# Layer 2's attention: a layer norm issued in halves between the counting exponentials, and v placed by two copies

## Chip, cores and metric

The kernel runs on one core of a Trainium2 chip. The metric is the device time of one execution in microseconds (us). The engines are PE (the matrix engine, with PEld for its weight loads), DVE (vector engine), ACT (scalar engine), POOL (GpSimd) and SP, which issues DMAs. Each engine works through its own queue in order.

## What is computed

Four layers, each a cross attention over a context and then a feed-forward part, act on `x` of 128 batches x 64 positions x 128 channels, all in float32. Each result is added to `x` with a tanh gate. Only layer 2's attention is touched by the change. Cut to what matters:

```python
q = (layernorm(x) @ Wq + bq)      # 16 heads of 8 channels
k = (ctx @ Wk + bk); v = (ctx @ Wv + bv)
attn = clip(einsum('bhqd,bhkd->bhqk', q, k) * 8 ** -0.5, -1e4, 1e4)
attn = softmax(attn)
attn = where(any(isnan(attn)), 1 / Nkv, attn)
x = x + tanh(g) * (einsum('bhqk,bhkd->bqhd', attn, v) @ Wo + bo)
```

The test for NaN runs over the whole tensor, so it is taken after all scores exist. The kernel forms it with an extra exponential of the raw scores, summed per row into `cnt`.

## The kernel before

**Tiling.** The 8192 tokens are 64 tiles of 128. Layer 2's attention works on 32 units of two tiles (`NP`, argument `u`) and 16 groups of four tiles (`NG`, argument `g`); a group is two units. An even unit is the first of its group.

**The steps of a group.** `statistics` (L786) takes mean and variance on DVE and, on POOL, four small operations that give `rr` (one over the deviation) and `nb` (minus mean times `rr`). `norm` (L798) applies both on ACT, one instruction for each of four tiles, into `xn`, of which there is a single buffer; then POOL adds the gated bias `b2` to the group's `x` in place. `transposes` (L806) turns `xn` on PE, `qk` (L813) forms q and k.

**The steps of a unit.** `spread` (L824, POOL) spreads k over head slots into `kb`; `scores` (L832, PE) fills two two-bank tiles `sc[0]` and `sc[1]`; `count` (L843, ACT) is the extra exponential, once for each of them; `clamp` (L848, DVE) clips each into `s`; `largest` (L855, DVE) takes the row maxima; `less` (L859, POOL, two halves) subtracts them; `power` (L863, ACT, two halves) is the softmax's exponential; `values` (L867, PE) forms v in `psv`; `place` (L876, DVE) copies v from there into a zeroed tile `vz`, in which each head's 8 columns sit at their own offset; `turn` (L886) transposes the exponentials on PE and copies them to `aT` on ACT; `heads` (L896, PE) multiplies them with `vz` and with a 0/1 tile that yields the row sums; `divide` (L913, DVE) makes the quotient.

**Order.** Steps of several units are interleaved by a list written out by hand, `PLAN` (L920). `period(i)` (L927) walks it once: an entry `("u", lag, f, ...)` calls `f` for unit `i + lag`, an entry `("g", lag, f)` calls it for group `(i + lag) / 2` when `i + lag` is even. The wrapper `InOrder` chains the instructions of every engine in the order in which they are issued, so an instruction that waits holds back all later ones of its engine. Before the change the list begins with count 0, clamp 1, clamp 0, count 1 of unit `i`, and ends with `("g", 6, statistics), ("g", 5, norm)`. So `statistics` of a group is the last step of an even unit, and its `norm` is the last step of the following odd unit. POOL's queue in an even unit is: the two `less`, the two multiplications of `spread`, the four small operations of `statistics`; in an odd unit: two `less`, two of `spread`, and the bias.

**Buffers.** One-bank PSUM tiles (L63) rotate over four banks: `psx`, `psq`, `psk`, `psv`, `psa` and `pso` share them. The two `sc` tiles (L66) are the only two of their kind, so the next unit's `scores` waits until `count` and `clamp` of the present one have read both.

**Around it.** Periods -6 to -2 run while layer 1 still works; the loop proper starts at -1. Layer 2's feed-forward part follows.

Of the kernel before, what the change touches and what calls it, by code (L numbers as in the profile page):

```python
# [9 lines left out]
F32 = mybir.dt.float32  # L10
# [3 lines left out]
ALU = mybir.AluOpType  # L14
AX = mybir.AxisListType

P = 128
# [37 lines left out]
def flamingo_kernel(ctx: ExitStack, tc: tile.TileContext, a: dict, out: bass.AP):  # L55
# [7 lines left out]
    def bank(name):  # L63
        return psum.tile([P, 512], F32, tag="one", name=name, bufs=4)
# [23 lines left out]
    x = const.tile([P, NT, DM], F32, name="x")  # L88
# [45 lines left out]
    def gated_bias(key):  # L134

        if key not in gbias:
            n = dict(b0=0, b1=1, b1f=5, b2=2, b3f=7, go=3)[key]
            gbias[key] = const.tile([P, DM], F32, name=f"gbias_{key}")
            dve.tensor_scalar(gbias[key], row[key], tg[:, n:n + 1], None, ALU.mult)
        return gbias[key]  # L140
# [5 lines left out]
    def bc(ap, axis, n):  # L146

        shape = list(ap.shape)
        shape.insert(axis, n)
        return ap.unsqueeze(axis).to_broadcast(shape)  # L150
# [21 lines left out]
    dve, actor, gps, mat, sp = engines = [InOrder(e) for e in (vec, act, pool, pe, nc.sync)]  # L172

    def opened(name, bufs=1, side=None):
        pl = tc.tile_pool(name=name, bufs=bufs, side=side, reuse_waits="tile")
        return pl
# [568 lines left out]
    def l2_cross(ahead):  # L745
# [4 lines left out]
        wk = early.enter_context(opened("l2x_0", 2, RIGHT))  # L750
# [6 lines left out]
        v = keep.tile([P, 4, 4, 2, 32], F32, name="vz")  # L757
# [17 lines left out]
        ps = bank("psvm")  # L775
# [4 lines left out]
        sg, su = [{} for _ in range(NG)], [{} for _ in range(NP)]  # L780
# [14 lines left out]
            gps.tensor_tensor(nb, mv[:, :, 0], rr, ALU.mult)  # L795
            gps.tensor_scalar(nb, nb, -1.0, None, ALU.mult)

        def norm(g):  # L798
            xn = sg[g]["xn"] = wk.tile([P, 4, P], F32, tag="xn", name=f"xn_l2x_{g}", bufs=1)
            for t in range(4):  # L800
                actor.activation(xn[:, t, :], x[:, 4 * g + t, :], AF.Identity, bias=sg[g]["nb"][:, t:t + 1],
                                 scale=sg[g]["rr"][:, t:t + 1])
            xs = x[:, 4 * g:4 * g + 4, :]
            gps.tensor_tensor(xs, xs, bc(gated_bias("b2"), 1, 4), ALU.add)

        def transposes(g):  # L806
            ps = bank(f"psx_l2x_{g}")
# [68 lines left out]
        def place(u):  # L876
            ps = su[u]["psv"]
            for r in range(2):
                rows = slice(r * 64, r * 64 + 64)
                flat = v[rows].rearrange("p b c j m -> p (b c j m)")  # L880
                for j in range(2):
                    o0 = 48 * j + 8 * r
                    dve.tensor_copy(flat.rearrange("p (n m) -> p n m", m=64)[:, :, o0:o0 + 8],
                                    ps[rows, 0:256].rearrange("p (n j d) -> p n j d", j=2, d=8)[:, :, j, :])

        def turn(u, t):  # L886
            aT = su[u]["aT", t] = wk2.tile([P, 8, P], F32, tag="aT", name=f"aT_l2x_{u}_{t}")
# [25 lines left out]
        def divide(u):  # L913
# [4 lines left out]


        PLAN = [  # L920
            ("u", 0, count, 0), ("u", 0, clamp, 1), ("u", 0, clamp, 0), ("u", 0, count, 1),
            ("u", -3, heads), ("g", 3, qk), ("u", -1, power, 0), ("u", -1, power, 1),
            ("u", -2, values), ("u", -2, turn, 0), ("u", 1, scores), ("u", -2, turn, 1), ("g", 4, transposes),
            ("u", 0, largest), ("u", 0, less, 0), ("u", 0, less, 1), ("u", -2, place), ("u", 2, spread),
            ("u", -3, divide), ("g", 6, statistics), ("g", 5, norm),
        ]
        def period(i):  # L927
            for kind, lag, f, *more in PLAN:
# [454 lines left out]
    def ahead(n):  # L1383
# [4 lines left out]
        l0_ffn(ahead(1)),  # L1388
        cross("l1x", 1, "b1", False, "l2f", ahead(2), NP - 6, mixed=True),
        l2_cross(ahead(3)),  # L1390
        l2_ffn(ahead(4)),
        l3_cross(ahead(5)),
# [105 lines left out]
```

## Time and profile before

| | |
|---|---|
| runs shown | 3167.32, 3157.87, 3159.76 us; median 3159.76 |
| profiled execution | 3154.1 us, of which the span from first to last instruction is 3152.3 |
| busy in the span | PE 2984.2 (95%), PEld 1972.2, DVE 1935.9 (61%), ACT 1564.0 (50%), POOL 1261.6 (40%) |
| mean granted TensorE clock | 0.986 |
| layer 2's attention, counts of unit 0 to unit 31 | starts at 1297.88 to 1568.81 us |
| one pair of units in its steady part | 17.96 us (count 0 of even units at 1330.48, 1348.46, 1366.42, ... 1528.04) |
| count 0 to count 0, even unit to odd, odd to even | 6.88 and 11.08 us |
| one count, one clamp, one `largest` | 1.02, 1.22, 2.29 us |
| one half of `less`, one power, one aT copy | 1.90, 1.05, 0.59 us |
| one place copy (64 partitions x 128) | 0.28 us |

Times in the trace count from the first instruction. A row of the timeline gives the start, the length, the engine, the operation with what it writes and reads, and in brackets how long the engine had been idle before it and whose result ended that. `x2` at its end means that two like instructions are merged into the row. Every instruction is recorded at one helper's line (L166), so rows are told apart by the names of their tiles: `junk` is a count, `s<-sc` a clamp, `m` the maxima, `s<-s,m` is `less`, `s<-s` a power, `kb` is `spread`, `xn` is `norm`, `vz` is `place`.

### The profile page before, as it was taken

What the parts mean: (1) busy time and instruction counts of PE and PEld (TensorE: products, weight loads), DVE (VectorE), ACT (ScalarE), POOL (GpSimd) and SP (SyncE); (2) the same over time, 40 slices, a digit from 0 to 9 for tenths busy, and PEclk for the clock granted to TensorE, in tenths of its full rate; (3) what the DMA queues carried; (4) which work ended last, traced back from release to release, by engine and by line L of the source; (5) the groups of instructions that cost most, each with busy time, mean ns of one, the idle gap of its engine ahead of it and who ended that gap; (6) DMA issues with size and microseconds to landing.
All of it is one profiled execution on the core that took longest, in us unless ns stands there. A gap on an engine that the chain in (4) does not pass through costs nothing. (4 is left out here: it accounts for less than half of the span.)

```text
span 3152.3 us, 80010 instructions
## 1 busy us (share of the span) xinstructions
PE 2984.2 (95%) x34018; PEld 1972.2 (63%) x34018; DVE 1935.9 (61%) x4558; ACT 1564.0 (50%) x2756; POOL 1261.6 (40%) x1439
## 2 busy tenths in 40 slices
PE   8999899999989999778879999999999999999998
PEld 7888544444448888555654444444446888888883
DVE  5666666666546667699964544544545666666664
ACT  5666432232236666688822332332325666666655
POOL 3434311111014444787714444444443333333343
PEclk9999999999999999899989999999999999999998
DMA  5000455655510000000025335435430000000001
GB/s 151 2 3 2 109 135 120 137 122 124 132 51 3 3 2 2 29 3 2 2 55 109 83 80 109 82 81 109 87 77 14 2 2 2 3 2 3 2 3 54
DMA packets 89512, 164.93 MB, mean 52 GB/s; under 512 B 8929, under 2 KB 20833, under 8 KB 88193
## 3 DMA queue, kind: packets, MB, share of 16 engines
q1 hardware_dynamic: 89154, 159.81, 22.6%
q8 instruction: 267, 4.37, 0.6%
q14 instruction: 91, 0.75, 0.1%
HBM read 154.00 MB, written 5.77 MB: 51 GB/s over the span
## 5 line engine op out<-in xcount | busy, mean ns | idle before, releaser
L166 PE MATMUL psgu_l2f<-xT_l2f,w_l2f 128*128 128x512 f32 x1088 | 512.7, 594 | 0.1
L166 POOL TENSOR_TENSOR h_l2f<-uw_l2f,sl_l2f 128x512 f32<-128x512 f32 x256 | 325.1, 1270 | 409.1 <-DVE uw_l2f L166 409.1
L166 DVE TENSOR_TENSOR uw_l2f<-psgu_l2f,wb_l2f 128x512 f32<-128x512 f32 x256 | 176.3, 689 | 361.6 <-ACT sl_l2f L166 361.6
L166 ACT ACTIVATE sl_l2f<-psgu_l2f 128x512 f32<-128x512 f32 x272 | 162.4, 597 | 465.9 <-PE psgu_l2f L166 465.8
L166 PE MATMUL psqkv_l0f<-xs_l0f,w_l0f 128*128 128x512 f32 (+1 forms) x1024 | 350.5, 599 | 3.5 <-DVE xs_l0f L166 3.5
L166 PEld LDWEIGHTS psgu_l2f<-xT_l2f,w_l2f 128*128 128x128 f32 x1088 | 202.1, 190 | 237.9 <-issue 222.6
L166 PE MATMUL psy_l2f<-h_l2f,w_l2f 128*128 128x512 f32 x544 | 277.6, 592 | 0.0
L166 PEld LDWEIGHTS psqkv_l0f<-xs_l0f,w_l0f 128*128 128x128 f32 (+1 forms) x1024 | 125.0, 164 | 188.9 <-issue 178.1
L166 POOL TENSOR_TENSOR at_l3x<-s_l3x,rec_l3x 128x1024 f32<-128x1024 f32 x64 | 121.8, 1904 | 164.3 <-DVE rec_l3x L166 153.6
L166 PEld LDWEIGHTS psy_l2f<-h_l2f,w_l2f 128*128 128x128 f32 x544 | 103.3, 190 | 129.6 <-issue 125.3
L166 POOL TENSOR_SCALAR rs_l0f<-mv_l0f 128x4 f32<-128x4 f32 x16 | 16.1, 1003 | 370.0 <-DVE mv_l0f L166 370.0
L166 DVE TENSOR_REDUCE den_l3x<-s_l3x 128x16 f32<-128x1040 f32 x64 | 79.1, 1235 | 130.1 <-ACT s_l3x L166 130.1
L166 POOL TENSOR_TENSOR x<-x,gbias_b 128x256 f32<-128x256 f32 (+1 forms) x80 | 68.0, 850 | 212.4 <-DVE ln_xn_l1x L166 109.1
L166 DVE TENSOR_TENSOR xs_l0f<-wb_l0f,xT_l0f 128x1024 f32<-128x1024 f32 x128 | 151.5, 1215 | 2.5 <-PE psqkv_l0f L166 1.1
L166 POOL TENSOR_TENSOR s_l2x<-s_l2x,m_l2x 128x1024 f32<-128x1024 f32 x64 | 120.4, 1903 | 53.4 <-DVE m_l2x L166 35.0
L166 PE MATMUL psq_l3x<-xT_l3x,w_l3x 128*128 128x256 f32 x512 | 135.3, 386 | 0.0
L166 PE MATMUL psk_l3x<-ctxT,w_l3x 96*128 96x256 f32 x512 | 132.4, 380 | 0.0
L166 PEld LDWEIGHTS pso_l3x<-w_l3x,oT_l3x 128*128 128x128 f32 x1024 | 125.9, 194 | 4.5 <-ACT oT_l3x L166 1.3
L166 DVE TENSOR_TENSOR s_l3x<-sc_l3x,maskf_m 128x512 f32<-128x512 f32 x128 | 82.4, 686 | 75.3 <-PE sc_l3x L166 75.3
L166 PE MATMUL pso_l3x<-w_l3x,oT_l3x 128*128 128x128 f32 x1024 | 126.4, 277 | 1.2 <-ACT oT_l3x L166 1.2
L166 PE MATMUL psv_l3x<-w_l3x,ctxT 97*64 97x256 f32 x1024 | 124.6, 385 | 0.0
L166 PE MATMUL psy_l0f<-mix_l0f,w_l0f 128*128 128x512 f32 x256 | 116.5, 609 | 2.0 <-DVE mix_l0f L166 2.0
(562 smaller groups left out, 6648.4 us busy)
## 6 DMA issues: line engine op xcount, KB each, us to landing
wb_l0f<-wrow_l0f SPq DMA_DIRECT2D x256, 256.0 KB, 5.7
wb_l2f<-wrow_l2f SPq DMA_DIRECT2D x128, 512.0 KB, 9.1
out_dram<-x SPq DMA_DIRECT2D x16, 256.0 KB, 2.6
w_l2f<-in_l2f_dram SPq DMA_DIRECT2D x1, 3280.0 KB, 10.3
w_l0f<-in_l0f_dram SPq DMA_DIRECT2D x1, 2088.0 KB, 27.5
w_l3x<-in_l3x_dram SPq DMA_DIRECT2D x1, 2049.0 KB, 8.3
x<-in_x_dram SPq DMA_DIRECT2D x1, 2048.0 KB, 18.9
ctxT<-in_ctxT_dram SPq DMA_DIRECT2D x1, 1536.0 KB, 23.7
```

The lines of the kernel that those rows point to most:

```text
L166: got = getattr(self.eng, op)(*args, **kwargs)
```

## The change

`norm` takes a unit instead of a group. It handles two of the group's four tiles in each call, takes the `xn` buffer in the first and adds the bias in the second. Its entry moves from the end of `PLAN` to a place between clamp 1 and clamp 0 at the start, with the lag 5 now counted in units; on ACT's queue that is between count 0 and count 1. In an odd unit `i` the call is for the first half of group `(i + 5) // 2`, in an even one for the second half. `place` copies both head parities with one instruction per half of the partitions, by a pattern that picks quarters 0 and 3 of each 64 columns.

```diff
-        def norm(g):
-            xn = sg[g]["xn"] = wk.tile([P, 4, P], F32, tag="xn", name=f"xn_l2x_{g}", bufs=1)
-            for t in range(4):
+        def norm(u):
+
+            g, half = divmod(u, 2)
+            if half == 0:
+                sg[g]["xn"] = wk.tile([P, 4, P], F32, tag="xn", name=f"xn_l2x_{g}", bufs=1)
+            xn = sg[g]["xn"]
+            for t in range(2 * half, 2 * half + 2):
                 actor.activation(xn[:, t, :], x[:, 4 * g + t, :], AF.Identity, bias=sg[g]["nb"][:, t:t + 1],
                                  scale=sg[g]["rr"][:, t:t + 1])
-            xs = x[:, 4 * g:4 * g + 4, :]
-            gps.tensor_tensor(xs, xs, bc(gated_bias("b2"), 1, 4), ALU.add)
+            if half == 1:
+                xs = x[:, 4 * g:4 * g + 4, :]
+                gps.tensor_tensor(xs, xs, bc(gated_bias("b2"), 1, 4), ALU.add)
...
-                flat = v[rows].rearrange("p b c j m -> p (b c j m)")
-                for j in range(2):
-                    o0 = 48 * j + 8 * r
-                    dve.tensor_copy(flat.rearrange("p (n m) -> p n m", m=64)[:, :, o0:o0 + 8],
-                                    ps[rows, 0:256].rearrange("p (n j d) -> p n j d", j=2, d=8)[:, :, j, :])
+
+                quarters = v[rows].rearrange("p b c j (a m) -> p (b c) (j a) m", a=2)
+                dve.tensor_copy(quarters[:, :, 0:4:3, 8 * r:8 * r + 8],
+                                ps[rows, 0:256].rearrange("p (n j d) -> p n j d", j=2, d=8))
...
-            ("u", 0, count, 0), ("u", 0, clamp, 1), ("u", 0, clamp, 0), ("u", 0, count, 1),
+            ("u", 0, count, 0), ("u", 0, clamp, 1), ("u", 5, norm), ("u", 0, clamp, 0), ("u", 0, count, 1),
...
-            ("u", -3, divide), ("g", 6, statistics), ("g", 5, norm),
+            ("u", -3, divide), ("g", 6, statistics),
```

## The prediction

> **What bounds the kernel now.** The granted clock and the busy table by stage come first: is the edited stage bound by the matrix engine, as its neighbours are? The rows give the stretch in us, its length, then the busy time of PE, PEld, DVE, ACT and POOL, the granted TensorE clock and DMA.
>
> ```profile
> 1400.00:1500.00 100.00, 81.60 (x1898) 60.30 (x1898) 90.64 (x142) 86.29 (x154) 80.58 (x72) 0.98 0.01 3
> ...
> 1800.00:1900.00 100.00, 97.04 (x255) 43.35 (x254) 46.75 (x151) 30.69 (x51) 45.90 (x40) 1.00 0.45 94
> ```
>
> In layer 2's attention (first row) four engines are 81 to 91% busy and none is full; in the expert layer behind it PE is at 97%. So a chain through several engines sets this stage, and what it loses is added to the end, as the next layer has no slack to absorb it. The stage's waits from 1330.48 to 1528.04 us (11 pairs of units) show where its chain turns; columns: total us, times, longest.
>
> ```profile
> ACT junk L166 <- DVE s_l2x L166: 23.0, 11, 2.2
> ...
> DVE s_l2x L166 <- ACT junk L166: 14.1, 11, 1.9
> ```
>
> Each happens once per pair: a counting exponential and a clamp that read the same scores tile never overlap. ACT's order of work over one pair (start, length) gives the rest; the row left out at each "..." is a read of an accumulator, kT or power.
>
> ```profile
> 1427.17 1.03 ACT L166 ACTIVATE junk<-sc_l2x 128x1024 bf16<-128x1024 f32 x1
> ...
> 1430.45 1.02 ACT L166 ACTIVATE junk<-sc_l2x 128x1024 bf16<-128x1024 f32 x1 [2.16 <-DVE s_l2x L166]
> ...
> 1431.46 0.68 ACT L166 ACTIVATE qT_l2x<-psq_l2x,bqs 128x512 f32<-128x512 f32 x1
> ...
> 1434.40 1.08 ACT L166 COPY aT_l2x<-psa_l2x 128x512 f32<-128x512 f32 x2
> 1435.74 1.07 ACT L166 COPY aT_l2x<-psa_l2x 128x512 f32<-128x512 f32 x2 [0.26 <-PE psa_l2x L166]
> 1436.70 1.65 ACT L166 ACTIVATE xn_l2x<-x,nb_l2x,rr_l2x 128x128 f32<-128x128 f32 x4
> 1438.25 1.01 ACT L166 ACTIVATE junk<-sc_l2x 128x1024 bf16<-128x1024 f32 x1
> ```
>
> Call T0 the first count of an even unit: 1420.30, next 1438.25, a period of **17.96 us** that repeats all 11 times. Its loop: count(even, 0) at T0, clamp(even, 0) 1.12 later (1421.42), DVE through largest, place, divide and statistics to clamp(odd, 1), whose end releases count(odd, 1) at T0+10.15, then ACT through qT, kT, power and the aT copies, then the four tiles of norm (1.55) to the next T0. DVE's own work is 16.74 of the 17.96; its 1.22 stall is clamp(even, 0) behind that late count.
>
> **What is removed.** Norm leaves the end of the odd unit: -1.55 on ACT's side of the loop. Place issues two copies of 64x256 for four of 64x128. Four take 0.98 (start to start about 0.235). An element costs 1.03 ns by the clamps of 1024 (1.215 us) against the score pass of 512 in layer 3 (0.686), so 128 more add 0.13: two of 0.37, the last 0.42, make 0.78. Saved: **0.20 us per unit**. No row has this 4-D pattern; were it no faster than now the saving is 0, were each copy twice its present length it is 0 as well. Where DVE waits anyway either is hidden.
>
> **What is added: a wait.** Norm now comes after count 0 in each unit, two tiles at a time. Half 1 lies in the even unit: its inputs are long there, and its 0.78 (half of 1.55) fits between count 0 and count 1 off the chain; the x bias on POOL then runs T0+1.95 to 3.25, before `less` at 4.88, so hidden. Half 0 lies in the **odd unit right behind the even unit whose end issued that group's statistics**; today a whole odd unit lies between. POOL's queue is in order, and the two `less`, then `spread`, stand before the four small operations that give nb:
>
> ```profile
> 1425.18 3.77 POOL L166 TENSOR_TENSOR s_l2x<-s_l2x,m_l2x 128x1024 f32<-128x1024 f32 x2 [2.10 <-DVE m_l2x L166]
> 1428.90 2.06 POOL L166 TENSOR_TENSOR kb_l2x<-kT_l2x,w_l2x 128x512 f32<-128x512 f32 x2
> 1431.05 0.23 POOL L166 TENSOR_SCALAR rs_l2x<-mv_l2x 128x4 f32<-128x4 f32 x1
> ...
> 1432.76 0.24 POOL L166 TENSOR_SCALAR nb_l2x<-nb_l2x 128x4 f32<-128x4 f32 x1
> ```
>
> ACT will reach norm near 1429 and nb ends at 1433.00. What this wait looks like is already once in the trace, at the stage's start, where nb's last operation began at 1296.05 (0.28 earlier) and a count stood behind norm:
>
> ```profile
> 1296.33 1.65 ACT L166 ACTIVATE xn_l2x<-x,nb_l2x,rr_l2x 128x128 f32<-128x128 f32 x4 [2.34 <-POOL nb_l2x L166]
> ```
>
> Queued behind the waiting norm on ACT are count(odd, 1), qT, kT, both powers and four aT copies; PE's next transposes wait for the qT bank, the next scores for count 1. This closes a **new loop**, by start-to-start gaps of the rows (DVE's at 1421.42 and 1422.75): T0 to clamp 0 1.12; to largest 1.33; to `less` 2.43; to `spread` 3.72; to rs 2.15; to nb's last operation 1.71; to norm 0.28; two tiles 0.78; count 1 to qT 1.01; kT 0.57; to power 0.47; two powers 1.90; first aT pair to second 1.34; to the next T0 0.96. Sum **19.77 us** against 17.96: +1.81 per pair. The norm's -1.55 and one place are outside this loop or already counted, so the saving on DVE only lengthens its waits.
>
> **PE's clock on top.** PE's last products before the wait (values) end at T0+10.79 now, 11.57 with half 1 in front; the transposes start when qT ends, at 15.26: 3.7 us of idle PE, where the trace has 1.10. The same busy table, cut at the boundaries at which the clock changes (3.41 us):
>
> ```profile
> 1457.90:1461.32 3.42, 1.66 (x37) 1.12 (x36) 3.32 (x4) 3.40 (x6) 1.32 (x2) 1.00 0.00 0
> 1461.32:1464.73 3.41, 3.41 (x66) 3.05 (x68) 3.33 (x9) 2.54 (x4) 3.41 (x2) 0.50 0.00 0
> ```
>
> 1.66 us of work in a window is followed by a window at half clock; 1.72 (the one from 1386.22) is not. [...] By the row half a window is enough: wherever the boundary falls, the gap leaves a window under 1.7. [...] The transposes and scores (1.09 and 1.12) then run partly at half speed and the second transposes start late: if half clock covers T0+15.0 to 18.4, scores end at 19.0 for 17.5 and the period is 20.7; from 14.25 to 17.7, 20.3; at worst 21.6. A period of six windows (20.48) keeps its phase, and on the side where a later window means a longer period it is drawn there. I take **20.5**, +2.52, bounds 19.77 and 21.6.
>
> **The sum.** Eleven pairs from unit 4 to 26: 11 x 2.52 = 27.7. Ramp: count 0 of unit 0 is 0.3 later, units 0 to 2 take the loop without aT copies, 17.4 for 14.15 (+3.2), 2 to 4 take 20.5 for 18.45 (+2.0): 5.5. After unit 26 no norm is left and DVE runs nearly full: 7 x 0.20 = -1.4. Together **+31.8 us**. The profiled run's own time is 3154.1 (span 3152.3): 3186. The median of the runs shown, 3159.76, lies 5.7 above that; on its level, 3191.
>
> **Rivals.**
> 1. The same wait with PE at full clock: 11 x 1.81 + 4.8 - 1.4 = +23.3: 3183. For it: the clock is free to fall elsewhere; against it: the 1.66 row.
> 2. A second half-clock window per pair, around the lone scores of the even unit (1.12 in 3.4 us): 21.6 per pair, 11 x 3.64 + 6.6 - 1.4 = +45: 3205. ACT's 3.9 us of slack before nb speak against.
> 3. **The loop is cut as drawn (faster).** Were nb there when ACT asks, half 0 would fill the 2.16 gap, DVE would be full at 16.74 - 0.40 = 16.34: 11 x -1.62 - 1 - 1.4 = -20: 3140. It needs nb by T0+9, and breaks even at 12.74 - 1.81 = 10.9; nb comes at 12.74. Only a POOL that runs `spread` later would do it, and its order is fixed.
> 4. Absorbed: the wait eats the 2.16 gap and the stall of 1.22, norm's 1.55 pays the rest: 3160. The closed loop of 19.77 speaks against: no slack is in it.
>
> **Chances.** Forecast 0.60, rival 1 0.20, rival 2 0.08, rival 3 0.07, rival 4 0.05. A change under 0.3% can't be told from none here. Faster 0.07, same 0.05, slower 0.88. The range 3176 to 3205 takes in rivals 1 and 2, with some room below for a ramp that hides more.
>
> **What would show it.** On ACT, xn in two pieces, in odd units with an idle of 3 to 4 us released by nb; T0 to T0 near 20.5; DVE's clamps waiting longer; half clock once a pair; vz copies 64 of 64x256 near 0.4 us. A period under 18 or no nb wait would make the forecast wrong.

## The result, and the profile after

| | before | changed |
|---|---|---|
| median of four runs, us | 3158.82 (3156.72 to 3167.32) | 3195.52 (3191.25 to 3197.85) |
| ratio, 95% interval | | 1.0105 [1.0089, 1.0120] |
| span of the profiled execution, us | 3152.3 | 3195.1 |
| count 0 to count 0 of even units, us | 17.96 | 20.51 |
| mean granted TensorE clock | 0.986 | 0.977 |

The kernel became 1.05% slower. The forecast was 3191 us on the level of the median before, with a range of 3176 to 3205. The busy table over eleven pairs (units 4 to 26; the kernel before first, then the changed one; columns as in the prediction) shows the loss: the stretch is 225.62 us where it was 197.56. DVE, ACT and POOL hold nearly the same work as before, so the time is in waits; PE's busy time is longer because its clock, 0.99 before, is 0.92.

```profile
1330.48:1528.04 197.56, 159.44 (x3614) 116.01 (x3608) 180.09 (x286) 167.88 (x299) 158.72 (x143) 0.99 0.01 3
...
1345.12:1570.74 225.62, 171.56 (x3615) 124.80 (x3608) 178.03 (x243) 165.72 (x299) 160.38 (x143) 0.92 0.01 2
```

The waits of the same stage (1336 to 1556 us; total, times, longest) have a new head. The two lines that turned the old loop, count and clamp waiting for each other, are replaced by these:

```profile
ACT xn_l2x L166 <- POOL nb_l2x L166: 46.4, 11, 4.5
DVE s_l2x L166 <- PE psa_l2x L166: 39.8, 11, 5.1
PEld psa_l2x L166 <- ACT qT_l2x L166: 35.1, 11, 4.5
```

ACT waits 4.2 us for nb once per pair. What stands behind it in the queue makes PE wait for the qT bank, and PE's late transposes make DVE's clamp wait: `s` has three buffers, so the clamp of unit `i + 1` writes where the second transposes of period `i`, which are those of unit `i - 2`, still read. The timeline of an odd unit shows ACT's wait, PE's wait behind it and the next count:

```profile
1419.61 0.88 ACT L166 ACTIVATE xn_l2x<-x,nb_l2x,rr_l2x 128x128 f32<-128x128 f32 x2 [4.19 <-POOL nb_l2x L166]
...
1420.39 1.00 ACT L166 ACTIVATE junk<-sc_l2x 128x1024 bf16<-128x1024 f32 x1
...
1421.39 0.67 ACT L166 ACTIVATE qT_l2x<-psq_l2x,bqs 128x512 f32<-128x512 f32 x1
...
1422.11 1.97 PE L166 MATMUL psa_l2x<-cst_t,s_l2x 128*128 128x128 f32 x8 [2.92 <-ACT qT_l2x L166]
...
1424.01 1.76 PE L166 MATMUL sc_l2x<-kb_l2x,qT_l2x 32*64 32x256 f32 x32
1424.33 1.07 ACT L166 COPY aT_l2x<-psa_l2x 128x512 f32<-128x512 f32 x2
...
1426.39 1.07 ACT L166 COPY aT_l2x<-psa_l2x 128x512 f32<-128x512 f32 x2 [0.99 <-PE psa_l2x L166]
...
1427.35 1.04 ACT L166 ACTIVATE junk<-sc_l2x 128x1024 bf16<-128x1024 f32 x1
```

In the kernel before, the same PE rows of an odd unit were:

```profile
1432.19 1.13 PE L166 MATMUL psa_l2x<-cst_t,s_l2x 128*128 128x128 f32 x8 [1.10 <-ACT qT_l2x L166]
...
1433.25 1.12 PE L166 MATMUL sc_l2x<-kb_l2x,qT_l2x 32*64 32x256 f32 x32
```

The eight transposes take 1.97 us where they took 1.13, and the 32 score products 1.76 where they took 1.12: PE is at half clock. Cut at the clock's boundaries, the busy table (the seventh figure behind the comma, after the five engines, is the clock) has a window with 0.64 us of PE work, and half clock in the next:

```profile
1418.55:1421.97 3.42, 0.64 (x17) 0.50 (x16) 3.38 (x4) 2.36 (x6) 2.37 (x4) 1.00 0.00 0
1421.97:1425.38 3.41, 3.27 (x38) 2.44 (x40) 1.32 (x2) 3.41 (x6) 2.31 (x3) 0.50 0.00 0
```

One such half-clock window comes in each of the eleven pairs, 20.48 us apart. Last, the copies of `place`, from the instructions that touch `vz` (min, median and max in ns):

```profile
L166 DVE COPY vz<-psv_l2x x64: 405/422/428, 1329.3 to 1641.2; 64x256 f32<-64x256 f32 x64
```

**Where the two traces part.** Of the 42.8 us between the two spans, 7.9 were there before the first moved `norm`, where both kernels issue the same work. This is variation of the execution, not the change: up to the same matmul shortly before the stage, the profiled executions of this study took from 1265.4 us (the kernel before) and 1265.9 (run d below) to 1273.4 (the changed kernel) and 1277.7 (run c2). Nearly all of the rest lies in layer 2's attention: 1.4 at its start, 5.3 in units 0 to 4, 28.1 in the eleven pairs, -0.3 from unit 26 to the last quotient. The last 0.4 come behind it.

### The profile page after: what moved, and what is told of

It is laid out like the page before. It is cut to its first block, busy times and chain, and to the rows that moved or that the text cites. A ratio compares the mean times of both kernels' runs of the same rounds, so it can differ in the third digit from the quotient of the medians.

```text
span 3195.1 us, 79944 instructions
## 1 busy us (share of the span) xinstructions
PE 3004.3 (94%) x34018; PEld 1985.4 (62%) x34018; DVE 1933.2 (61%) x4494; ACT 1561.6 (49%) x2756; POOL 1262.6 (40%) x1439
## 4 chain that ended last, share of the span: by engine, by line
PE 79%; DVE 10%; POOL 4%; ACT 4%; issue 2%; DMA 0%; DVEq 0%; POOLq 0%; ACTq 0%
PE psgu_l2f L166 11%; PE psqkv_l0f L166 11%; PE psy_l2f L166 5%; PE psv_l3x L166 4%; PE psy_l0f L166 4%; PE pso_l3x L166 4%; PE psq_l3x L166 4%; PE psk_l3x L166 3%; PE sc_l3x L166 2%; PE psa_l3x L166 2%; PE o_l3x L166 2%; PE psq_l1x L166 2%; PE psv_l1x L166 2%; PE psk_l1x L166 2%; PE pso_l1x L166 2%
## 5 line engine op out<-in xcount | busy, mean ns | idle before, releaser
L166 PE MATMUL psa_l2x<-cst_t,s_l2x 128*128 128x128 f32 x512 | 81.5, 309 | 53.8 <-ACT qT_l2x L166 36.5
```

The lines of the kernel that those rows point to most:

```text
L166: got = getattr(self.eng, op)(*args, **kwargs)
```

## The experiments

The theory is the prediction's: ACT's wait for nb closes a loop through POOL's queue, and PE's gap halves its clock on top. The rivals are that the new copies are at fault, that norm between the counts costs by itself, and that the clock lies off the path. "Pair" is the time from count 0 of one even unit to the next, taken from each profile in the steady part. The kernel before had a median of 3160.48 us beside runs a, b, c and d, and of 3155.91 beside c2, e and g, so runs of the two sets are compared by their ratios.

| run | pair, us | median, us | ratio to before, 95% interval |
|---|---|---|---|
| before | 17.96 | | 1 |
| changed | 20.51 | 3195.52 | 1.0105 [1.0089, 1.0120] |
| a_norm_moved_only | 19.38 and 21.65 in turn (one of 20.32), mean 20.50 | 3192.15 | 1.0104 [1.0087, 1.0121] |
| b_two_copies_only | 17.53 to 17.56 (one of 17.91) | 3151.10 | 0.9977 [0.9963, 0.9991] |
| c_busy_in_gap | 19.94 | 3190.36 | 1.0098 [1.0079, 1.0116] |
| c2_busy_in_gap_short | 19.43 | 3184.24 | 1.0084 [1.0065, 1.0103] |
| e_spread_last | 17.57 | 3160.56 | 1.0008 [0.9996, 1.0021] |
| g_norm_later_four_copies | 16.69 | 3148.52 | 0.9976 [0.9966, 0.9985] |
| d_norm_later | 16.42 (one of 16.79) | 3142.63 | 0.9949 [0.9933, 0.9965] |

**Each part alone.** Run a gives the changed kernel its four copies back; run b is the kernel before with the two copies.

```diff
# a, on the changed kernel (b is the reverse on the kernel before)
-                quarters = v[rows].rearrange("p b c j (a m) -> p (b c) (j a) m", a=2)
-                dve.tensor_copy(quarters[:, :, 0:4:3, 8 * r:8 * r + 8],
-                                ps[rows, 0:256].rearrange("p (n j d) -> p n j d", j=2, d=8))
+                flat = v[rows].rearrange("p b c j m -> p (b c j m)")
+                for j in range(2):
+                    o0 = 48 * j + 8 * r
+                    dve.tensor_copy(flat.rearrange("p (n m) -> p n m", m=64)[:, :, o0:o0 + 8],
+                                    ps[rows, 0:256].rearrange("p (n j d) -> p n j d", j=2, d=8)[:, :, j, :])
```

> The changed kernel with v placed in four copies again: only the norm is moved. Theory (the loop through nb sets the pair, place lies outside it): count 0 of even units every 20.48 us as in the changed kernel, the four copies cost at most 0.2 us in each of the last 7 units: about +1.4 us on the changed kernel's 3195, ratio to before 1.011 to 1.012. Rival (the wider copies with their pattern of four dimensions bring the loss): the pair falls to 17.96 us or less, time 3160 or less.

> The kernel before with the two copies alone, norm where it was. Theory (before the change one place per pair is part of the loop count 0, clamp 0, largest, place, divide, statistics, clamp 1, count 1): 17.96 becomes 17.83 to 17.76 us, the last 7 units save up to 0.2 us each: -3 to -4 us, ratio about 0.999. Rival (copies bring the loss): above 1.003.

The moved norm alone brings the whole loss, and the copies alone a gain: the copies are cleared. The time of a agrees with the expectation within its interval. It was expected that its pairs keep one length; they alternate, because the half clock falls differently on every second pair: 6.8 us of it in one, none in the next. The busy table of a long pair and of the short one behind it:

```profile
1468.97:1490.61 21.64, 16.64 (x324) 12.06 (x324) 16.37 (x27) 15.21 (x28) 14.74 (x14) 0.84 0.01 2
1490.61:1509.99 19.38, 14.42 (x352) 10.47 (x340) 16.54 (x27) 14.92 (x28) 14.41 (x13) 1.00 0.01 2
```

The odd unit of a short pair, at full clock, shows what the loop is without the clock's part:

```profile
1364.59 1.39 PE L166 MATMUL psa_l2x<-cst_t,s_l2x 128*128 128x128 f32 x8
...
1364.69 2.04 ACT L166 COPY aT_l2x<-psa_l2x 128x512 f32<-128x512 f32 x4
```

The four aT copies follow each other without the 0.26 us gap of before, since the second transposes start before the first copies are out: the bank that they need is free by then. This pair is 19.38 us.

Run b's pair fell by 0.43 us, not by the 0.13 to 0.20 expected; its ratio allows -3 to -12 us. The kernel before, then run b, each in an odd unit:

```profile
1433.79 0.99 DVE L166 COPY vz<-psv_l2x 64x128 f32<-64x128 f32 x4
...
1435.05 1.09 PE L166 MATMUL psa_l2x<-cst_t,s_l2x 128*128 128x128 f32 x8 [0.67 <-ACT aT_l2x L166]
```

```profile
1420.02 0.85 DVE L166 COPY vz<-psv_l2x 64x256 f32<-64x256 f32 x2
...
1420.63 2.12 ACT L166 COPY aT_l2x<-psa_l2x 128x512 f32<-128x512 f32 x4
...
1421.01 1.06 PE L166 MATMUL psa_l2x<-cst_t,s_l2x 128*128 128x128 f32 x8 [0.41 <-DVE vz L166]
```

DVE saves 0.14 us per unit (two copies take 0.84 to 0.85, four took 0.98 to 0.99), and one unit's share of that shows in the loop: from count 0 of the even unit to count 1 of the odd one it takes 10.02 us, before 10.16. The larger part is on ACT's side: from count 1 of the odd unit to the next count 0 it takes 7.51 us, before 7.80. The second transposes now start right behind the end of `place`; before, `place` had ended 0.27 us earlier and they started right behind the end of the first aT copy. By the semaphores in the traces the first four of the eight wait for ACT and the last four for DVE in the kernel before, and the other way round in run b, so the two programs seem to hand out the two free banks in opposite order. How much of the 0.29 us comes from that order and how much from the shorter copies is not shown.

**The clock.** Runs c and c2 give PE work that nobody reads in its gap (the fill). They compute all else as the changed kernel does.

```diff
# c2; c has range(9)
+            if u % 2 and u < NP - 2:
+                for _ in range(5):
+                    mat.matmul(ps[:, 256:512], lhsT=ident, rhs=cst_t[:, 0:256], start=True, stop=True)
             su[u]["psv"] = ps
```

> The changed kernel with nine matmuls of 128x256 that nobody reads behind the values of each odd unit (about 2.4 us at full clock), in PE's gap before qT; nothing else is changed. Theory (a window of 3.41 us with under 1.7 us of work halves the clock once per pair, and that lengthens the loop from 19.77 to 20.48): clock back at 1.00 in the pairs, pair 19.8 to 19.9 us, some 7 us less than the changed kernel, ratio to before about 1.008. Rival (the clock lies off the path, the loop is 20.48 long anyway): pair stays at 20.48, or longer because PE has more to do.

> As c_busy_in_gap with five matmuls instead of nine: there they ran 4.15 us and ended 1 us after qT, so PE was late by its own load; five should take 2.3 us and fit into the gap. Theory (full clock alone takes the pair to the warm 19.39): pair 19.4 us, clock full, about 12 us less than the changed kernel: 3180 to 3186. Rival (19.39 in a_norm_moved_only came from something else): pair 19.9 us or more.

In c the fill ran 4.15 us, not the 2.4 expected, and outlasted the gap, so its pair is 0.5 us longer than c2's. In c2 it fits; the third row is the busy table over its eleven pairs:

```profile
1438.28 2.42 PE L166 MATMUL psv_l2x<-cst_t 128*128 128x256 f32 x10
1438.78 0.88 ACT L166 ACTIVATE xn_l2x<-x,nb_l2x,rr_l2x 128x128 f32<-128x128 f32 x2 [4.19 <-POOL nb_l2x L166]
...
1348.25:1561.97 213.72, 183.66 (x3722) 133.48 (x3718) 179.04 (x243) 164.82 (x299) 159.98 (x143) 1.00 0.01 2
```

ACT waits for nb as long as in the changed kernel, yet the clock stays full in all the pairs and a pair is 19.43 us. So more work on PE takes 1.08 us from each pair: the half clock lies on the path with that much. Run a agrees: its short pairs, at full clock without any fill, take 19.38 us. The rest of the loss, 19.43 against 17.96, is the wait. The whole time shows less: the ratio is 1.0084 for 1.0105, and the two intervals overlap. About 3 us are lost again behind unit 26, where the fill goes on though no norm waits any more (units 26 to 30 take 33.6 us for 30.7). The 1.08 us rest on the pairs of the profiles.

**The wait.** Run e changes only the order of POOL's queue: nb comes before `spread`. Run d moves norm and what follows it (`transposes`, `qk`) one unit later, so that nb is old when ACT asks; norm still stands between the counts. Run g is d with four copies, written as in a.

```diff
# e, on the changed kernel
-            ("u", 0, largest), ("u", 0, less, 0), ("u", 0, less, 1), ("u", -2, place), ("u", 2, spread),
-            ("u", -3, divide), ("g", 6, statistics),
+            ("u", 0, largest), ("u", 0, less, 0), ("u", 0, less, 1), ("u", -2, place),
+            ("u", -3, divide), ("g", 6, statistics), ("u", 2, spread),
# d, on the changed kernel, three lags of PLAN
-            ... ("u", 5, norm), ... ("g", 3, qk), ... ("g", 4, transposes),
+            ... ("u", 4, norm), ... ("g", 2, qk), ... ("g", 3, transposes),
```

> The changed kernel with spread moved behind statistics, so that POOL makes nb before the two multiplications of spread; the norm stays where the change put it. Theory (nb's place in POOL's queue sets the pair): nb comes 2.15 us sooner, the loop at full clock, 19.39 us by run a_norm_moved_only, becomes 17.2 to 17.6, PE's gap shrinks to about 1.6 us and the clock stays full: some 3 us under a pair of the changed kernel, time 3150 to 3163. Rival (the wait is long because of something else than POOL's order, such as statistics on DVE): pair stays above 19 us, time above 3180.

> The changed kernel with norm one unit later (lag 4), transposes at lag 3 and qk at lag 2: the first half now comes in the even unit after next to statistics, when nb is a whole odd unit old; norm still stands between the counts. Theory (only the wait for nb costs): no idle before xn, DVE full at 16.34 us a pair, about -20 us on the kernel before: 3135 to 3142, ratio 0.993 to 0.995. Rival (norm between the counts costs by itself, since it delays count 1 and with it the next scores): pair above 17.96 us, ratio above 1.000.

> d_norm_later with v placed in four copies. Theory (there DVE is full, so the copies count): pair 16.41 + 0.3 = 16.7 us, ratio to before 0.996 to 0.997, 3 to 6 us more than d_norm_later. Rival (the copies matter by the bank that they free, not by DVE's time): pair 16.4 or above 17.0 us.

Run e, POOL and ACT of one odd unit, and PE's transposes behind it:

```profile
1424.95 0.24 POOL L166 TENSOR_SCALAR nb_l2x<-nb_l2x 128x4 f32<-128x4 f32 x1
...
1425.16 2.05 POOL L166 TENSOR_TENSOR kb_l2x<-kT_l2x,w_l2x 128x512 f32<-128x512 f32 x2
1425.23 0.88 ACT L166 ACTIVATE xn_l2x<-x,nb_l2x,rr_l2x 128x128 f32<-128x128 f32 x2 [2.34 <-POOL nb_l2x L166]
...
1427.73 1.13 PE L166 MATMUL psa_l2x<-cst_t,s_l2x 128*128 128x128 f32 x8 [1.08 <-ACT qT_l2x L166]
```

With nb ahead of `spread` (the `kb` row) ACT's idle falls from 4.19 to 2.34 us, PE's gap from 2.92 to 1.08, and the transposes run at full clock. The pair falls by 2.94 us: 1.85 of the wait and 1.08 of the clock. More than half of the wait is still there. The pair is 0.39 us shorter than before the change, but the time can't be told from that of the kernel before.

Run d, one pair's two norm calls and DVE's clamps:

```profile
1421.14 2.33 DVE L166 TENSOR_SCALAR s_l2x<-sc_l2x 128x1024 f32<-128x1024 f32 x2
...
1421.73 0.91 ACT L166 ACTIVATE xn_l2x<-x,nb_l2x,rr_l2x 128x128 f32<-128x128 f32 x2
...
1429.16 2.35 DVE L166 TENSOR_SCALAR s_l2x<-sc_l2x 128x1024 f32<-128x1024 f32 x2
...
1429.71 0.88 ACT L166 ACTIVATE xn_l2x<-x,nb_l2x,rr_l2x 128x128 f32<-128x128 f32 x2
```

No bracket stands behind the norm: ACT does not wait for nb. Both clamps of each unit run as one piece, where one had waited for a count in every pair. DVE is now the bound, at 160.52 of 164.53 us over ten pairs:

```profile
1346.25:1510.78 164.53, 141.95 (x3280) 103.23 (x3280) 160.52 (x221) 151.95 (x271) 144.58 (x131) 1.00 0.01 3
```

So norm between the counts is not at fault; that rival falls. Run g, over its ten pairs:

```profile
1348.37:1515.23 166.86, 142.35 (x3280) 103.23 (x3280) 163.21 (x261) 152.22 (x272) 144.55 (x131) 1.00 0.01 3
```

Where DVE is full the copies cost as DVE time: DVE's busy time is 2.69 us more than in d over ten pairs, and a pair is 16.69 against 16.42, which is 0.27 for two units, 0.14 each. The ratio of g, 0.9976, lies above the 0.996 to 0.997 that was expected; its distance to d's is about 8 us where 3 to 6 were expected, but the two intervals nearly touch, so this size is not settled. **Run d is faster than both kernels**, by 0.5% on the one before and by 1.5% on the changed one (0.9949 over 1.0105).

## Why the prediction was right, step by step

- **Direction and cause.** "A new loop" through nb sets the pair: shown by a, in which nothing but norm is moved, by e, in which nb comes earlier and ACT's wait and the pair shrink together, and by d, in which nb is there in time and the loss turns into a gain.
- **The loop up to count 1.** From T0 to count 1 of the odd unit the links summed to 13.52 us; measured 7.44 + 6.11 = 13.55.
- **The loop behind it.** The link "first aT pair to second 1.34" was too long. At full clock the four copies take 2.04 us in one piece, and a pair is 19.38 to 19.43, not 19.77. The 1.34 held a wait of the second transposes for the bank of the first aT copy. In a, c2 and e they start before that copy does, so they no longer wait for its bank; that they take the bank of `place` instead, as in run b, is likely but not shown. A gap taken from the old trace keeps a wait that the new order may remove.
- **PE's clock.** Mis-sized the other way, 0.71 in the sum and 1.08 by c2. The idle stretch is 2.92 us, not 3.7, since `heads` in the odd unit now starts 1.00 us late, behind DVE's quotient. Even so a half-clock window came in each pair; the window before it held 0.49 to 0.70 us of PE work in the eleven pairs. The row of 1.66 us, on which the prediction relied, pointed the right way, but it is no sharp limit (see the end). This error and that of the link before it cancel: that a pair came out at the 20.5 of the forecast is in part luck.
- **A pair in step with the clock's window.** It held in the changed kernel (20.48 us from one half-clock window to the next) but not in run a, where long and short pairs (21.65 and 19.38 us) alternate about nearly the same mean. So the settling can't be counted on.
- **The copies.** One copy takes 0.422 us, as forecast, but two of them 0.84, not 0.78: saved are 0.14 us per unit. Off the loop this did not matter.
- **Start and end.** Start 1.4 for 0.3; there ACT waited 4.32 us for nb, with qT and kT behind it. Units 0 to 2 17.35 for 17.4, units 2 to 4 20.51 for 20.5. From unit 26 on -0.3 for -1.4: unit 26 still holds half a norm (26 to 28 took 16.46 us for 15.98), and only the later pairs are shorter (28 to 30 14.23 for 15.09).
- **The sum.** 34.5 us in the stage by the two traces (1.4 + 5.3 + 28.1 - 0.3), 31.8 forecast; 36.7 by the medians of four runs each.
- **The rival "faster".** Its sum was sound: with nb there in time a pair of 16.34 and 3140 us were worked out, and run d has 16.42 and 3142.63. It was rightly held unlikely for this change, where nb comes late. It named another order of POOL as the only way to it; run e shows that this is not enough, and run d that norm one unit later is.

## What to carry to other kernels

When a step is moved ahead in an order written by hand, count how many steps now lie between it and the one that makes its inputs, on the producer's queue and not on its own: here the free slot on ACT was real, and the input was the last thing in POOL's queue. Close the loop with start-to-start gaps from the trace, and ask of each gap whether it is work or a wait that the new order would lift. A gap that opens on PE is to be priced with the clock that follows it in the trace: here half clock came behind the gap of 2.92 us in each pair and cost 1.08 us, while behind a gap of 2.80 us in a short pair of run a, and of 1.08 us in run e, the clock was full.

## What had not been expected of the hardware

PE's clock halved behind windows of 3.41 us with up to 1.66 us of PE work, and the busy time alone does not tell which windows. In layer 2's attention (1325 to 1600 us) of the kernel before, the full-clock windows with 1.14, 1.54, 1.65 and 1.66 us of PE work were followed by half clock; those with 1.57 (from 1591.02), 1.72 and 1.80 and all with more kept it full. In the changed kernel the windows with 0.23 to 0.70 us were followed by half clock; the next larger one, 1.78, and all above it kept it full. In run a a window with 1.53 us, transposes alone, kept it as well. So the prediction's pair of 1.66 and 1.72 is no limit: 1.53 and 1.57 kept the clock and 1.54, 1.65 and 1.66 lost it. What decided there is not shown. Run a, that window and the next:

```profile
1473.42:1476.83 3.41, 1.53 (x12) 1.29 (x12) 3.33 (x7) 3.15 (x7) 2.91 (x2) 1.00 0.03 5
1476.83:1480.25 3.42, 3.27 (x99) 2.38 (x100) 3.40 (x11) 0.75 (x2) 3.25 (x5) 1.00 0.02 5
```

Work that nobody reads, 2.4 us per pair, made a pair 1.08 us shorter. And in run b, where only DVE's copies were touched, ACT's side of the loop became 0.29 us shorter per pair, about as much as both units' copies save on DVE together; there PE's second transposes wait for `place` instead of an aT copy.
